# An encoder-decoder layer: two score pieces ahead of a visit's values, and the values' bank in a ring of eight

## The chip, the core and the metric

The kernel runs on one NeuronCore of one Trainium2 chip. The metric is the device time of one launch in microseconds. All arithmetic is fp32. The engines that matter here are TensorE (PE in the profile, with its weight loads as PEld), VectorE (DVE), ScalarE (ACT), GpSimd (POOL), and the DMA queue that SyncE (SP) issues.

## What is computed

One transformer layer with an encoder over a short context (2 sequences of 77 rows) and a decoder over 2 sequences of 2048 rows, width 512, 16 heads of 32. The part that the change touches is the decoder's causal self-attention:

```python
yn = _ln(y, dec_n1_s, dec_n1_b)
y = y + _mha(yn, yn, dec_sa_in_w, dec_sa_in_b, dec_sa_out_w, dec_sa_out_b, sb)
# inside _mha, for each head:
scores = einsum('bhqd,bhkd->bhqk', q, k) / sqrt(hd) + bias     # bias holds the causal mask
attn = softmax(scores, axis=-1)
out = einsum('bhqk,bhkd->bhqd', attn, v)                       # then out @ w_out.T + b_out
```

After it come cross-attention to the encoder's 77 rows and a feed-forward part of width 2048. The kernel does these last two in a second stage, and computes several of the large products there and the key and value projections by a seven-product scheme of half-size blocks.

## The kernel before, in words

**Units.** Self-attention is cut into units `(b, m, g, t)`: batch `b` (2), block `m` of 512 rows (4), group `g` of four heads (4), and tile `t` of 128 query rows in the block (4). A unit has `i = 4m + t` key tiles before its own, so it works on `i + 1` tiles of 128 keys: 1 to 4 in block 0, 5 to 8 in block 1, 9 to 12 in block 2, 13 to 16 in block 3. Units run in the order of the tuple.

**Pieces and visits.** `pieces(i)` (L315) cuts the key tiles of a unit into pieces of at most four. The main loop (L1730 to L1756) takes up to two pieces of one unit at a time; this text calls one such turn of the loop a visit. A unit of block 1 has one visit, a unit of blocks 2 and 3 has two. In block 3 both visits have two pieces; in block 2 the second visit has one.

**What a visit does.** The steps are, in program order:

- `turn(pair)` (L410): for every key tile ("load" in the code) four 128x128 transposes of the probabilities, one per head, into one PSUM bank (PE, L424), and a copy of that bank to one of eight SBUF tiles `pts`. The first half of the copies goes to ACT (L430), the second half to DVE (L428). One exponential is emitted behind the fourth load, and one at the end.
- `slot(n + 1)`, at a unit's last visit only: the jobs that a table has for the next unit: projections of queries, keys and values of the next block, the output projection `out_job` of the block before, and norms. A job is typically 8 or 16 matmuls.
- one score piece (`scores`, L357): four matmuls in row groups, one per head, each into its own bank (PE, L374), and then four evictions by DVE that write the raw scores to SBUF and take their maximum (L383), or add the bias for the last two tiles of a unit (L390). After a unit's last piece DVE makes the negated maximum `nm` (L399), and the four exponentials of the unit are put into a list, `late_exps`.
- `exps(k)`: emits up to `k` exponentials from that list to ACT (L404); `k` is 2 in block 1 and 1 in blocks 2 and 3.
- `values` (L435): for every key tile of the visit four matmuls in column groups (PE, L441).
- the remaining score pieces that are allowed (`while may_score()`).

Which scores are allowed follows from `may_score`: the probabilities of unit `n` overwrite those of unit `n - 2`, so a piece of unit `n + 2` may be scored as soon as unit `n` has been transposed that far. In block 3 that is two pieces at each visit, and the last piece of unit `n + 2` belongs to the second visit of unit `n`.

**Order on the engines.** The schedule is written out by hand: each engine's instructions run in the order in which the code emits them, and semaphores hold an instruction until its operands are ready. So an instruction that waits on ACT holds all that stands behind it on ACT.

**PSUM.** There are eight banks. Seven of them go round in `bank()` (L179): transposes, jobs and scores take the next one in turn, whatever it was used for last, and wait until its last reader is done. The eighth, bank 7, belongs to `values`: the four tiles `t` of a group accumulate there over all their key tiles, and when the last is done the whole bank (128x512) is copied to an SBUF tile `oT` (L447), by DVE for blocks 1 to 3. Six `oT` tiles go round; `out_job` reads four of them per block.

Of the kernel before, what the change touches and what calls it, by code (L numbers as in the profile page):

```python
# [12 lines left out]
ALU = mybir.AluOpType  # L13
# [4 lines left out]
P = 128  # L18
B, T, S, D = 2, 2048, 77, 512
H, HD, DFF = 16, 32, 2048  # L20
NC = D // P
NF = DFF // P
HC = P // HD
MB = 512
NMB = T // MB
TB = MB // P
# [28 lines left out]
def tile_encoder_decoder(ctx: ExitStack, tc: tile.TileContext, ins, out):  # L55
    nc = tc.nc
    x, src = ins["x"], ins["ctx_1024"]
# [101 lines left out]
    with (  # L159
# [14 lines left out]
        oT_all = ac.tile([P, 6, TB * P], F32, name="oT")  # L174
        bo = ac.tile([P, D], F32, name="row_dec_sa_out_b")
        psum = ps.tile([P, 8, 512], F32, name="psum")
        count = {"bank": 0, "banks": 7, "pts": 0, "oT": 0, "mm": 0}

        def bank():  # L179

            i = count["bank"] % count["banks"]
            count["bank"] += 1
            return psum[:, i, :]

        def in_turn(what, tile):
            i = count[what] % tile.shape[1]
            count[what] += 1
            return tile[:, i, :]

        def rows4(r):  # L190
            return slice(r * HD, (r + 1) * HD)
# [54 lines left out]
        def out_job(b, m, t):  # L246
            def run(w):
                x1 = xr.pop((b, m, t))
                mm = bank()
                for c in range(NC):  # L250
                    nc.tensor.matmul(  # L251
                        mm, ots[b, m, c][:, ts(t, P)], w[:, c, :], start=(c == 0), stop=(c == NC - 1)
                    )
                nc.vector.tensor_tensor(x1, mm, x1, ALU.add)
                nc.sync.dma_start(y1[b][m][:, t, :], x1)

            return lambda: big_w("o"), run, False
# [10 lines left out]
        def residual(b, m, t):  # L268
            residual_load(b, m, t)
            residual_add(b, m, t)  # L270
# [139 lines left out]
        def turn(pieces):  # L410

            first = units[pieces[0][0]][1] == 0
            loads = []
            for n, k0, kn in pieces:
                ks = range(k0, k0 + kn)
                if first:
                    loads += [[(n, k, r) for k in ks] for r in range(HC)]
                else:
                    loads += [[(n, k, r) for r in range(HC)] for k in ks]
            for o, load in enumerate(loads):  # L420
                pt = bank()
                pts = in_turn("pts", pts_all).rearrange("p (x q) -> p x q", q=P)
                for x, (n, k, r) in enumerate(load):
                    nc.tensor.transpose(pt[:, ts(x, P)], state[n]["p"][r][:, k], ident)  # L424
                    got[n, k, r] = pts[:, x, :]
                w = len(load) * P
                if o % 2 if first else o >= (len(loads) + 1) // 2:
                    nc.vector.tensor_copy(pts[:, : len(load), :], pt[:, :w])  # L428
                else:
                    nc.scalar.copy(pts[:, : len(load), :], pt[:, :w])  # L430
                if not first and o == min(3, len(loads) - 1):
                    exps(1)
            exps(HC if first else 1)

        def values(n, k0, kn):  # L435
            b, m, g, t = units[n]
            i = m * TB + t
            for k in range(k0, k0 + kn):
                ot = psum[:, 7, :].rearrange("p (t q) -> p t q", q=P)
                for r in range(HC):  # L440
                    nc.tensor.matmul(  # L441
                        ot[rows4(r), t, :], vv[:, k, ts(g * HC + r, HD)], got.pop((n, k, r)),
                        start=(k == 0), stop=(k == i),
                    )
                if t == TB - 1 and k == i:
                    o = ots[b, m, g] = in_turn("oT", oT_all)
                    (nc.vector.tensor_copy if m else nc.scalar.copy)(o, psum[:, 7, :])  # L447

        ri_of = [const.tile([P, RB], F32, name=f"ri{i}") for i in range(2)]
        for t in ri_of:  # L450
# [617 lines left out]
        for x, (b, m) in enumerate(blocks):  # L1068
            u = x * NU
            first = m == 0  # L1070

            if first:
                jobs[max(u - 5, -1)].append(q_job(b, m, 0))
                jobs[max(u - 4, -1)].append(k_job(b, m, 0))
                for t, at in enumerate((u + 1, u + 2, u + 3, u + 4) if x else (-1, 1, 3, 4)):
                    jobs[at].append(v_job(b, m, t))
                jobs[u - 1 if x else 0].append(q_job(b, m, 1))
                jobs[u if x else 2].append(k_job(b, m, 1))
                for g, at, then in ((2, 3, 4), (3, 5, 6)) if x else ((2, 6, 7), (3, 8, 9)):
                    jobs[u + at].append(q_job(b, m, g))  # L1080
                    jobs[u + then].append(k_job(b, m, g))
            else:
                (late if x == 1 else light)[u - 5].append(lambda b=b, m=m: token_sums(b, m))
                todo = {
                    -5: "q0", -4: "k1 k6", -3: "k7 k4", -2: "k2 k5", -1: "k3 v1", 0: "v6 v7", 1: "v4 v2", 2: "q1",
                    3: "v5 v3", 4: "q2", 5: "q3",
                } if x > 1 else {
                    -4: "q0 k1", -3: "k6 k7", -2: "k4 k2", -1: "k5 k3", 0: "v1 v6", 1: "v7 v4 v2", 2: "q1",
                    3: "v5 v3", 4: "q2", 5: "q3",
                }  # L1090
                for at, names in todo.items():
                    for name in names.split():
                        i = int(name[1])
                        jobs[u + at].append(q_job(b, m, i) if name[0] == "q" else part_job(name[0], b, m, i))
            if x == 0:
                jobs[NU + 5].append(fold_job())
            for t in range(TB):
                end = x == len(blocks) - 1
                jobs[u + NU + (2 if end else 7) + t].append(out_job(b, m, t))
                if not end:  # L1100
                    light[u + NU + 6 + t].append(lambda b=b, m=m, t=t: residual(b, m, t))
                elif t < 2:
                    light[u + NU - 1].append(lambda b=b, m=m, t=t: residual(b, m, t))
                if x:
                    held = x == 1 and t >= 2
                    light[u - NU + 5 + t].append(lambda b=b, m=m, t=t, held=held: norm_load(b, m, t, held))
                    ahead[u - NU + 6 + t].append(lambda b=b, m=m, t=t: norm_stats(b, m, t))
                    ahead[u - NU + 6 + t].append(lambda b=b, m=m, t=t: norm_center(b, m, t))
                    turned_at = 10 + t // 2 if x == 1 else u - NU + 7 + t
                    light[turned_at].append(lambda b=b, m=m, t=t: norm_turn(b, m, t))  # L1110
            for g in range(NC):
                apart = not (x == len(blocks) - 1 and g >= NC - 2)
                d = spread(b, m, g) if apart else divide(b, m, g)
                for k in range(4 if apart else 2):
                    light[u + g * TB + TB + k].append(lambda d=d: next(d, None))
                at = u + g * TB - 3
                light[max(at, -1)].append(lambda b=b, m=m, g=g: load_bias(b, m, g))
# [602 lines left out]
        def score_next():  # L1720
            n, k0, kn = stream[at[0]]
            scores(n, k0, kn)
            scored_to[n] = k0 + kn
            at[0] += 1
# [5 lines left out]
        while i < len(stream):  # L1730
            n = stream[i][0]
            pair = [p for p in stream[i : i + 2] if p[0] == n]
            while scored_to.get(n) != size[n]:
                score_next()
            while any(u == n for u, _ in late_exps):
                exps(1)
            ends = pair[-1][1] + pair[-1][2] == size[n]
            if ends:
                for f in ahead[n + 1]:
                    f()  # L1740
            turn(pair)
            if n == end - 2:
                for _, k0, _ in pair:
                    feed(k0 + 4)
            turned_to[n] = pair[-1][1] + pair[-1][2]
            if ends and n + 1 < end:
                slot(n + 1)
            if may_score():
                score_next()
            exps((0, 2, 1, 1)[units[n][1]])  # L1750
            for p in pair:
                values(*p)
            while may_score() and (len(pair) > 1 or units[n][1] == 0):
                score_next()
            i += len(pair)
# [2 lines left out]
        for t in (2, 3):  # L1758
            residual_load(*blocks[-1], t, pts_all[:, 2 * t - 3, :])
        late_loads()  # L1760
        count.update(bank=0, banks=4)
        side = cross(1)
        slot(end)
        for s in range(4):
# [58 lines left out]
```

## Time and profile before

| | us |
|---|---|
| median of three runs (2784.79 to 2785.24) | 2784.84 |
| the profiled execution | 2785.57 |
| its span, first to last instruction | 2783.8 |

| engine | busy us | share of the span | instructions |
|---|---|---|---|
| PE | 2757.1 | 99% | 26294 |
| PEld | 2137.0 | 77% | 26294 |
| DVE | 1885.9 | 68% | 5412 |
| ACT | 1439.6 | 52% | 2761 |
| POOL | 915.2 | 33% | 777 |

A row of the timeline holds the start and the length in us, the engine, the line of the kernel, the operation with what it writes and reads, a count where like instructions are merged, and in brackets how long the engine was idle before it and what released it. Matmuls overlap in their pipeline and their ends are modelled, so PE's busy time hides short waits. What a group of matmuls costs is read from its start to the start of the next group. Self-attention takes the time to about 1700 us of the span, the second stage the rest.

### The profile page before, as it was taken

What the parts mean: (1) busy time and instruction counts of PE and PEld (TensorE: products, weight loads), DVE (VectorE), ACT (ScalarE), POOL (GpSimd) and SP (SyncE); (2) the same over time, 40 slices, a digit from 0 to 9 for tenths busy, and PEclk for the clock granted to TensorE, in tenths of its full rate; (3) what the DMA queues carried; (4) which work ended last, traced back from release to release, by engine and by line L of the source; (5) the groups of instructions that cost most, each with busy time, mean ns of one, the idle gap of its engine ahead of it and who ended that gap; (6) DMA issues with size and microseconds to landing.
All of it is one profiled execution on the core that took longest, in us unless ns stands there. A gap on an engine that the chain in (4) does not pass through costs nothing. (4 is left out here: it accounts for less than half of the span.)

```text
span 2783.8 us, 66824 instructions
## 1 busy us (share of the span) xinstructions
PE 2757.1 (99%) x26294; PEld 2137.0 (77%) x26294; DVE 1885.9 (68%) x5412; ACT 1439.6 (52%) x2761; POOL 915.2 (33%) x777
## 2 busy tenths in 40 slices
PE   9999999999999999999999999999999999999998
PEld 5577776677666566676677667898989898989898
DVE  5676587788887578687788895555555646464645
ACT  3544455656666556666656665434444444444431
POOL 1501134400100412212300002364646474746456
PEclk9999999999999999999999999999999999999999
DMA  7423345421112521233211004574748575656475
GB/s 224 140 88 110 111 129 161 128 59 38 38 55 58 142 76 55 89 100 103 96 55 40 25 32 138 182 236 155 230 155 233 179 224 162 221 163 222 147 227 182
DMA packets 282252, 362.45 MB, mean 130 GB/s; under 512 B 39073, under 2 KB 156625, under 8 KB 281811
## 3 DMA queue, kind: packets, MB, share of 16 engines
q1 hardware_dynamic: 281938, 358.18, 42.0%
q8 instruction: 208, 3.41, 0.5%
q14 instruction: 106, 0.86, 0.1%
HBM read 314.49 MB, written 43.59 MB: 129 GB/s over the span
## 5 line engine op out<-in xcount | busy, mean ns | idle before, releaser
L404 ACT ACTIVATE pp<-pp,nm 128x128 f32<-128x128 f32 (+15 forms) x512 | 612.1, 1202 | 143.8 <-DVE nm L399 139.3
L383 DVE TENSOR_SCALAR_CACHE_REDUCE pp<-psum 128x512 f32<-128x512 f32 (+3 forms) x1024 | 558.9, 591 | 59.1 <-PE psum L374 57.4
L424 PEld LDWEIGHTS psum<-ident,pp 128*128 128x128 f32 x4352 | 475.8, 142 | 110.0 <-DVE pp L383 56.0
L430 ACT COPY pts<-psum 128x512 f32<-128x512 f32 (+3 forms) x592 | 300.9, 576 | 474.1 <-PE psum L424 342.8
L424 PE MATMUL psum<-ident,pp 128*128 128x128 f32 x4352 | 538.3, 278 | 7.6 <-ACT nT L310 2.3
L428 DVE COPY pts<-psum 128x512 f32<-128x512 f32 (+2 forms) x544 | 330.1, 660 | 65.8 <-PE psum L424 65.1
L374 PE MATMUL psum<-kT,q 32*128 32x512 f32 (+3 forms) x2560 | 358.7, 574 | 3.8 <-DVE pp L383 1.9
L441 PEld LDWEIGHTS psum<-pts,vv 128*32 128x32 f32 x8704 | 225.8, 110 | 126.0 <-issue 115.6
L1523 PE MATMUL psum<-pp 128*128 128x128 f32 x2560 | 304.5, 276 | 1.9 <-POOL pp L936 1.6
L1523 PEld LDWEIGHTS psum<-pp 128*128 128x128 f32 x2560 | 296.3, 192 | 8.6 <-issue 2.8
L441 PE MATMUL psum<-pts,vv 128*32 128x128 f32 x8704 | 279.5, 275 | 2.4 <-DVE pts L428 1.7
L936 POOL TENSOR_TENSOR pp<-pp 128x512 f32<-128x512 f32 x159 | 212.7, 1354 | 128.1 <-DMA pp<-in_dec_ff_wT_dram 68.9
L1494 PE MATMUL psum<-vv,pp 128*128 128x256 f32 x1024 | 236.2, 381 | 0.0
L374 PEld LDWEIGHTS psum<-kT,q 32*128 32x128 f32 x2560 | 122.8, 183 | 122.8 <-issue 79.6
L1494 PEld LDWEIGHTS psum<-vv,pp 128*128 128x128 f32 x1024 | 190.5, 190 | 25.6 <-issue 0.5
L390 DVE CUSTOM_DVE_ANT_0 pp<-psum,bias 128x256 f32<-128x256 f32 (+1 forms) x512 | 196.1, 411 | 15.7 <-PE psum L374 15.6
L1507 DVE TENSOR_TENSOR kT<-kT,psum 128x512 f32<-128x512 f32 x96 | 65.8, 686 | 190.7 <-PE psum L1494 190.6
L1494 PE MATMUL psum<-nT,pp 128*128 128x256 f32 x768 | 174.1, 380 | 0.0
L1510 ACT ACTIVATE kT<-kT,vecs 128x256 f32<-128x256 f32 x192 | 87.0, 501 | 156.7 <-DVE kT L1507 156.0
L1494 PEld LDWEIGHTS psum<-nT,pp 128*128 128x128 f32 x768 | 144.3, 190 | 20.2 <-issue 1.6
L469 POOL TENSOR_TENSOR oT<-rirows,oT 128x512 f32<-128x512 f32 x30 | 38.3, 1275 | 368.9 <-DMA rirows<-rec 214.2
L1531 ACT COPY oT<-psum 128x128 f32<-128x128 f32 x56 | 14.9, 267 | 239.2 <-PE psum L1523 239.2
(242 smaller groups left out, 3908.5 us busy)
## 6 DMA issues: line engine op xcount, KB each, us to landing
pp<-w_d SPq DMA_DIRECT2D x520, 256.0 KB
pp<-in_dec_ff_wT_dram SPq DMA_DIRECT2D x112, 256.0 KB
wqk<-in_dec_sa_in_wT_dram SPq DMA_DIRECT2D x76, 256.0 KB
bias<-tzg SPq DMA_DIRECT2D x128, 128.0 KB
pp<-wo_d SPq DMA_DIRECT2D x56, 256.0 KB
vv<-in_enc_ff_wT_dram SPq DMA_DIRECT2D x8, 1024.0 KB
xr<-in_x_dram SPq DMA_DIRECT2D x32, 256.0 KB
vv<-y SPq DMA_DIRECT2D x32, 256.0 KB
```

The source lines that it names most:

```text
L374: nc.tensor.matmul(banks[r][:, : kn * P], q[rows4(r), ts(t, P)], kT[rows4(r), g, k0 * P : (k0 + kn) * P], start=True, stop=True,)
L383: nc.vector.tensor_scalar(p[:, k0 : k0 + far], s[:, :far], 1.0, None, ALU.mult, ALU.max, accum_out=st["mx"][:, r, c : c + 1],)
L390: nc.vector.tensor_tensor_reduce(p[:, k0 + far : i + 1], s[:, far:kn], near[:, 2 - (kn - far) :], 1.0, LOWEST, ALU.add, ALU.max, accum_out ...
L404: nc.scalar.activation(p, p, AF.Exp, bias=nm, accum_out=to)
L424: nc.tensor.transpose(pt[:, ts(x, P)], state[n]["p"][r][:, k], ident)
L428: nc.vector.tensor_copy(pts[:, : len(load), :], pt[:, :w])
L430: nc.scalar.copy(pts[:, : len(load), :], pt[:, :w])
L441: nc.tensor.matmul(ot[rows4(r), t, :], vv[:, k, ts(g * HC + r, HD)], got.pop((n, k, r)), start=(k == 0), stop=(k == i),)
L936: engine.tensor_tensor(out, a, b, ALU.subtract)
L1494: nc.tensor.matmul(mm[:, ts(f, TOK)], a[:, c, ts(f, P)], b[:, c, :], start=fresh and f == 0 and c == 0, stop=c == 1, skip_group_check=True,)
L1510: nc.scalar.activation(dst[:, e, :], src[:, e, :], AF.Relu, bias=vec("dec_ff1_b", f + e))
L1523: nc.tensor.matmul(psum[:, bank_i, ts(col, P)], lhs[:, c, :], w[:, c, :], start=fresh and k in (0, 3) and c == 0, stop=c == 3, skip_group_ ...
```

## The change

There are four edits and a few that follow from them.

1. **Two score pieces in a row.** At a visit with two pieces in blocks 1 to 3, up to two score pieces are emitted ahead of `exps(k)` and `values`, where there was one. The other visits keep one.
2. **The ring has eight banks, and the values take theirs from it.** `values` now takes a whole visit. It takes the bank that has been longest in the ring, sums that visit's key tiles there, and gives the bank back to the end of the ring once the eviction is emitted. Block 0 still holds one bank for the four tiles of a group, and copies it as 128x512.
3. **Sums beside PSUM.** In blocks 1 to 3 a visit's sum is evicted as 128x128: the first visit of a unit by a copy on ACT into the `oT` tile, the second by DVE, which adds it there. One unit per block, `(g, t) = (2, 0)`, holds its bank over both visits and is copied once, on ACT.
4. **Copies of a visit with eight loads.** ACT takes six of the eight copies (all but loads 4 and 6), where it took four. The exponential that stood behind the fourth load stands behind the eighth. Other lengths stay as they were.

The output projections of a block other than the last in its batch move one slot earlier (slots 6 to 9 of the next block where they were 7 to 10), and so does the residual's load and its addition on POOL.

```diff
-        count = {"bank": 0, "banks": 7, "pts": 0, "oT": 0, "mm": 0}
+        count = {"pts": 0, "oT": 0, "mm": 0}
+        ring = list(range(8))
 
         def bank():
-            i = count["bank"] % count["banks"]
-            count["bank"] += 1
-            return psum[:, i, :]
+            ring.append(ring.pop(0))
+            return psum[:, ring[-1], :]
...
                 w = len(load) * P
-                if o % 2 if first else o >= (len(loads) + 1) // 2:
+                if o % 2 if first else o in (4, 6) if len(loads) == 8 else o >= (len(loads) + 1) // 2:
                     nc.vector.tensor_copy(pts[:, : len(load), :], pt[:, :w])
                 else:
                     nc.scalar.copy(pts[:, : len(load), :], pt[:, :w])
-                if not first and o == min(3, len(loads) - 1):
+                if not first and o == (7 if len(loads) == 8 else min(3, len(loads) - 1)):
                     exps(1)
             exps(HC if first else 1)
 
-        def values(n, k0, kn):
+        sums_held = {}
+
+        def values(pair):
+            n, k0, _ = pair[0]
             b, m, g, t = units[n]
             i = m * TB + t
-            for k in range(k0, k0 + kn):
-                ot = psum[:, 7, :].rearrange("p (t q) -> p t q", q=P)
+            k1 = pair[-1][1] + pair[-1][2]
+            whole = m == 0
+            key = (b, m, g) if whole else n
+            begun = key in sums_held
+            if not begun:
+                sums_held[key] = ring.pop(0)
+            v = sums_held[key]
+            ot = psum[:, v, ts(t, P)] if whole else psum[:, v, :P]
+            keep = t < TB - 1 if whole else (g, t) == (2, 0) and k1 <= i
+            for k in range(k0, k1):
                 for r in range(HC):
                     nc.tensor.matmul(
-                        ot[rows4(r), t, :], vv[:, k, ts(g * HC + r, HD)], got.pop((n, k, r)),
-                        start=(k == 0), stop=(k == i),
+                        ot[rows4(r)], vv[:, k, ts(g * HC + r, HD)], got.pop((n, k, r)),
+                        start=k == k0 and (whole or not begun), stop=k == k1 - 1 and (whole or not keep),
                     )
-                if t == TB - 1 and k == i:
-                    o = ots[b, m, g] = in_turn("oT", oT_all)
-                    (nc.vector.tensor_copy if m else nc.scalar.copy)(o, psum[:, 7, :])
+            if keep:
+                return
+            if (b, m, g) not in ots:
+                ots[b, m, g] = in_turn("oT", oT_all)
+            o = ots[b, m, g]
+            if whole:
+                nc.scalar.copy(o, psum[:, v, :])
+            elif k0 == 0 or begun:
+                nc.scalar.copy(o[:, ts(t, P)], ot)
+            else:
+                nc.vector.tensor_tensor(o[:, ts(t, P)], ot, o[:, ts(t, P)], ALU.add)
+            ring.append(sums_held.pop(key))
...
-                jobs[u + NU + (2 if end else 7) + t].append(out_job(b, m, t))
+                out_at = u + NU + (2 if end else 7 if m == NMB - 1 else 6) + t
+                jobs[out_at].append(out_job(b, m, t))
                 if not end:
-                    light[u + NU + 6 + t].append(lambda b=b, m=m, t=t: residual(b, m, t))
+                    (light if x else late)[out_at - 1].append(lambda b=b, m=m, t=t: residual(b, m, t))
...
-            if may_score():
-                score_next()
+            for _ in range(2 if len(pair) > 1 and units[n][1] else 1):
+                if may_score():
+                    score_next()
             exps((0, 2, 1, 1)[units[n][1]])
-            for p in pair:
-                values(*p)
+            values(pair)
             while may_score() and (len(pair) > 1 or units[n][1] == 0):
                 score_next()
...
-        count.update(bank=0, banks=4)
+        assert len(ring) == 8
+        ring[:] = range(4)
```

## The prediction

> **What bounds the kernel now.** I read the page's engine busy times first, then the busy times by stretches of 100 us, the waits of PE's weight loads, and the timeline of blocks 2 and 3.
>
> ```profile
> PE 2757.1 (99%) x26294; PEld 2137.0 (77%) x26294; DVE 1885.9 (68%) x5412; ACT 1439.6 (52%) x2761; POOL 915.2 (33%) x777
> 800.00:900.00 100.00, 99.78 (x1262) 70.51 (x1263) 74.95 (x241) 65.89 (x107) 1.27 (x1) 1.00 0.16 44
> PEld psum L424 <- DVE pp L383: 56.0, 93, 0.8
> PEld psum L374 <- ACT pts L430: 3.7, 19, 0.2
> ```
>
> PE bounds it, and the change removes no matmul. So it can only win or make waits of PE. These hide inside the modelled matmul times, so I compare each PE group's start-to-start time with the shortest of its kind. In self-attention the excess sums to 65 us of 1700, nearly all of it in 91 places of over 0.15 us (the first at 23.6, the last at 1697.3). That is the most there is to win. Here is block 2:
>
> ```profile
> 424.92 0.71 PE L374 MATMUL psum<-kT,q 32*128 32x256 f32 x8
> 425.56 0.86 PE L441 MATMUL psum<-pts,vv 128*32 128x128 f32 x24
> 425.65 0.43 DVE L390 CUSTOM_DVE_ANT_0 pp<-psum,bias 128x256 f32<-128x256 f32 x1
> 426.36 3.71 PE L424 MATMUL psum<-ident,pp 128*128 128x128 f32 x32
> 427.35 1.26 ACT L404 ACTIVATE pp<-pp,nm 128x1152 f32<-128x1152 f32 x1 [3.97 <-DVE nm L399]
> 428.61 2.02 ACT L430 COPY pts<-psum 128x512 f32<-128x512 f32 x4
> 430.00 1.81 PE L374 MATMUL psum<-kT,q 32*128 32x512 f32 x8
> 430.68 0.30 PEld L374 LDWEIGHTS psum<-kT,q 32*128 32x128 f32 x4 [0.20 <-ACT pts L430]
> 431.74 1.95 PE L441 MATMUL psum<-pts,vv 128*32 128x128 f32 x64
> 433.62 1.14 PE L374 MATMUL psum<-kT,q 32*128 32x512 f32 x8
> 434.70 1.97 PE L424 MATMUL psum<-ident,pp 128*128 128x128 f32 x16
> 434.78 0.69 DVE L383 TENSOR_SCALAR_CACHE_REDUCE pp<-psum 128x512 f32<-128x512 f32 x1 [1.06 <-PE psum L374]
> 437.23 1.28 DVE L428 COPY pts<-psum 128x512 f32<-128x512 f32 x2
> ```
>
> A unit's last piece is scored at 424.92, ahead of its visit's values. DVE evicts it, and the first exponential of that unit starts at 427.35, when `nm` is there. It stands on ACT ahead of the next turn's copies, whose banks filled from 426.36 on, so they start at 428.61. At 430.68 two of the next score matmuls still wait for a bank that ACT has not copied, and the values start at 431.74, 1.74 us behind that piece instead of the 1.08 us that the piece at 433.62 takes.
>
> In block 3 this does not happen, because the last piece comes behind the values and `exps` ahead of them:
>
> ```profile
> 706.64 1.30 PE L441 MATMUL psum<-pts,vv 128*32 128x128 f32 x40
> 707.87 0.93 PE L374 MATMUL psum<-kT,q 32*128 32x384 f32 x8
> 709.18 0.29 DVE L383 TENSOR_SCALAR_CACHE_REDUCE pp<-psum 128x128 f32<-128x128 f32 x1
> 709.42 2.06 ACT L430 COPY pts<-psum 128x512 f32<-128x512 f32 x4 [5.54 <-PE psum L424]
> 711.73 1.90 ACT L404 ACTIVATE pp<-pp,nm 128x1920 f32<-128x1920 f32 x1 [0.25 <-DVE nm L399]
> 723.74 4.63 PE L424 MATMUL psum<-ident,pp 128*128 128x128 f32 x32
> 724.39 0.42 DVE L383 TENSOR_SCALAR_CACHE_REDUCE pp<-psum 128x256 f32<-128x256 f32 x1
> 727.47 2.00 ACT L404 ACTIVATE pp<-pp,nm 128x2048 f32<-128x2048 f32 x1 [0.93 <-DVE nm L399]
> 728.30 1.27 PE L374 MATMUL psum<-kT,q 32*128 32x512 f32 x8
> 729.47 1.99 ACT L404 ACTIVATE pp<-pp,nm 128x2048 f32<-128x2048 f32 x1
> 729.50 1.95 PE L441 MATMUL psum<-pts,vv 128*32 128x128 f32 x64
> 731.39 1.14 PE L374 MATMUL psum<-kT,q 32*128 32x512 f32 x8
> 732.46 3.33 PE L424 MATMUL psum<-ident,pp 128*128 128x128 f32 x28
> ```
>
> ACT copies at 709.42 as soon as banks fill, and the exponential (711.73) comes behind the copies. What is lost here is small: the turn at 723.74 waits 0.9 us for DVE's banks (4.56 to 728.30, against 3.64 from 426.36 to 430.00).
>
> The Trainium skill (Perfetto Trace Analysis, Identifying the Most-Contended Engine) judges PE's headroom by LDWEIGHTS busy time and calls matmul busy time a bad measure. By it the stretch above has 30% to win and a gain of hundreds of us would be open. The rows disagree: a run of values without a wait (64 matmuls, 729.50 to 731.39) repeats to 0.01 us, so I keep 65 us as the ceiling.
>
> **The change, part by part.**
>
> *Two score pieces in a row, block 3.* At the second visit of unit n both pieces of unit n + 2, the last one included, now come ahead of `exps(1)`. The list is empty then (three of the unit's four exponentials go out at each first visit), so the first exponential of n + 2 is emitted there, ahead of the next turn's copies, as in block 2. Of eight loads six copies are ACT's, and the next two pieces take the turn's eight banks in order, so they wait for these copies. The chain from the first piece A of a second visit to the values V of the next visit, for 16 key tiles:
>
> - A's start to its first eviction 1.16 (433.62 to 434.78), four evictions 2.45 (434.78 to 437.23), the last piece's evictions to the exponential 3.08 (724.39 to 727.47), the exponential 2.00;
> - four copies to the bank of head 3, 2.06, and 0.05 to the matmul (430.63 to 430.68); then two pieces of 1.07, behind which copies 5 and 7 (2 x 0.52) are just in time: 2.14.
>
> The sum is 12.9 us. Applied to the row at 424.92, with one piece: 0.73 + 1.70 + 1.26 + 2.02 + 0.05 + 1.07 = 6.83, measured 6.82. PE's own work on that way is two pieces 2.14, values of six tiles 1.45 (between 1.23 for five at 706.64 and 1.88 for eight), the turn 3.64, two pieces 2.14: 9.4. So PE waits 3.5 us. In the same way n + 2 of 15 tiles: last piece 2.55 (709.18 to 711.73), exponential 1.9, 12.3 against 8.9, 3.4 us; of 14 (last piece of two tiles 1.70, 425.65 to 427.35; exponential 1.8): 11.4 against 9.4, 2.0 us; of 13 (pieces of three and two tiles, 0.95 + 1.9 + 1.7 + 1.7 + 4.25): 10.5 against 8.9, 1.6 us. A batch has 4, 4, 3 and 3 of these: 14.0 + 13.6 + 6.0 + 4.8 = 38 us, two batches **+77**. Jobs do not cover it: they stand between the turn and A, ahead of the chain.
>
> *The visit after.* ACT then runs three exponentials, the 0.27 us sum copy and the second visit's copies. PE reaches its pieces after values and a turn of five to eight loads. I work this out to 0.5 to 1.7 us of wait where slot n + 1 has no job (9 slots in all), else a 3.5 us job covers it: **+10**. Block 1 emits two exponentials behind the fresh `nm`; jobs cover that, except at slot 10, which loses its output projection to slot 6: **+5**.
>
> *What goes.* The second of two pieces in a row waits for the first one's bank, because the ring has seven:
>
> ```profile
> 403.48 3.04 PE L374 MATMUL psum<-kT,q 32*128 32x512 f32 x16
> 1458.29 3.03 PE L374 MATMUL psum<-kT,q 32*128 32x512 f32 x16
> 1461.25 0.98 PE L424 MATMUL psum<-ident,pp 128*128 128x128 f32 x7
> 465.13 2.71 PE L374 MATMUL psum<-kT,q 32*128 32x512 f32 x8
> 467.77 0.43 PE L441 MATMUL psum<-pts,vv 128*32 128x128 f32 x8
> 469.30 5.37 PE L424 MATMUL psum<-ident,pp 128*128 128x128 f32 x32
> 474.60 0.71 PE L374 MATMUL psum<-kT,q 32*128 32x512 f32 x4
> ```
>
> 2.96 us instead of 2.14, 14 times (the first and last rows): 11. Where DVE is late (465.13, 1.6 us; 469.30, 1.7 us), its lead and its relief help. Of block 2's 29 us in both batches I take 21 as gone (the 0.7 us waits like that at 430.00 stay), of block 3's 10 all, of block 1's 11 half: **-36**. The bounds are -11 (the ring alone) and -65 (all).
>
> *Copies and sums.*
>
> ```profile
> L1531 ACT COPY oT<-psum 128x128 f32<-128x128 f32 x56 | 14.9, 267 | 239.2 <-PE psum L1523 239.2
> L1539 DVE TENSOR_TENSOR oT<-psum,oT 128x128 f32<-128x128 f32 x56 | 15.7, 281 | 0.0
> L447 DVE COPY oT<-psum 128x512 f32<-128x512 f32 x24 | 16.4, 685 | 1.0 <-PE psum L441 1.0
> ```
>
> 72 visits have eight loads, so 144 copies (0.64 us on DVE, half of the pair at 437.23; 0.52 on ACT) move: DVE -92, ACT +75. The sums put 96 x 0.267 = 26 on ACT, 60 x 0.281 = 17 on DVE, and take 24 x 0.685 = 16 from it. No engine gets full, and what these cost in order is in the chains, so they count nothing more. A visit's sum needs the bank of head 0 of its first piece, evicted 1.8 us after that piece starts; the values start after 2.14. If DVE is late there, PE waits that long.
>
> *Moved jobs.* The output projections, residual loads on SP's queue and POOL's additions go together one slot earlier and keep their lead of a slot; only slot 10 is priced, above.
>
> Sum: 77 + 10 + 5 - 36 = +56 on the profiled execution's 2785.57, which stands 0.7 above the median: **2841**.
>
> **Rivals.**
>
> - *Faster.* PE does not wait in block 3, because the first exponential's `nm`, with DVE relieved, is early enough for the copies. Then only the -36 stays: 2749. For it: block 2 pays only 0.7 us in the same place. Against it: the chain fits that place to 0.01 us, and it has no DVE copy in it. It decides below 1.3 us a visit (36/28), where I have 2.75. The Trainium skill (PSUM — Partial Sum Buffer, Engine vs sequencer instructions) says that ScalarE's queue is strict FIFO. By it 2841, without it 2749; the copies at 428.61 agree with it.
> - *ACT binds in block 3.* The delay never drains, so the second wait (1.1 us) comes at all 32 units, not at 9, and only 20 us is gained: 77 + 35 + 5 - 20, 2882. For it: a 16-tile unit has 4 x 2.0 + 12 x 0.52 + 0.27 = 14.5 us on ACT against 15.5 on PE. Against it: most units have 3.5 us of jobs.
> - *No difference.* The waits are about half as long and balance the gain.
>
> **Numbers.** Forecast 0.65, at 2800 (all 65 won) to 2875; ACT binds 0.10; faster 0.20; no difference 0.05. Faster or slower by 0.2% (5.6 us) is about what can be told here, so 0.20, 0.05 and 0.75. The range goes from 2750, with half of the faster case, to 2880.
>
> **What would show it.** In block 3's timeline: an exponential of a new unit ahead of six ACT copies at each first visit, and score pieces of 4 to 5.5 us in a row instead of 2.14, released by ACT pts L430; that wait of PE's weight loads well above 3.7. Groups of 16 score matmuls at 2.14 in block 2. I am wrong if block 3 shows its copies ahead of the exponentials, or if PE's pieces wait for DVE instead.

## The result, and the profile after

| kernel | median us | ratio to before (95%) | block 1 | block 2 | block 3 |
|---|---|---|---|---|---|
| before | 2784.79 | | 407.3 | 469.7 | 526.7 |
| after | 2858.26 | 1.0264 (1.0253 to 1.0275) | 405.6 | 461.9 | 604.2 |

The medians are those of five executions each. The change makes the kernel 73.5 us slower; the forecast was 56 us slower. A block's column is the time from the first transpose of its units to the first of the next block's, summed over the two batches, in the profiled execution (2854.09 us, the fastest of the five, 68.5 above that of before). Blocks 1 and 2 gain 9.5 us, and block 3 loses 77.5.

The engine line and the waits of PE's weight loads after the change (tile and line, then what released them: sum in us, count, and the longest one):

```profile
PE 2794.0 (98%) x26294; PEld 2197.1 (77%) x26294; DVE 1807.6 (63%) x5304; ACT 1530.9 (54%) x3001; POOL 915.3 (32%) x777
```

```profile
PEld psum L452 <- DVE pp L383: 71.9, 97, 1.5
PEld psum L374 <- ACT pts L430: 54.3, 193, 2.0
PEld psum L424 <- DVE pp L383: 17.9, 53, 0.8
```

DVE lost 78 us of work and ACT got 91; the prediction's terms add up to 91 and 101. The wait of the score matmuls' weight loads for ACT's copies rose from 3.7 to 54.3 us, which is the wait named in advance. The first row, values (now L452) that wait for an eviction of scores, was named but not priced; experiment 1 shows that it costs PE next to nothing.

Block 3's timeline shows the chain, once with a unit of 16 key tiles next (645.84) and once with one of 13 (667.40):

```profile
645.84 2.04 PE L374 MATMUL psum<-kT,q 32*128 32x512 f32 x16
647.81 1.52 PE L452 MATMUL psum<-pts,vv 128*32 128x128 f32 x48
649.25 4.18 PE L424 MATMUL psum<-ident,pp 128*128 128x128 f32 x32
652.32 0.17 DVE L399 TENSOR_REDUCE nm<-mx 128x4 f32<-128x20 f32 x1
652.59 2.00 ACT L404 ACTIVATE pp<-pp,nm 128x2048 f32<-128x2048 f32 x1 [6.95 <-DVE nm L399]
654.59 3.00 ACT L430 COPY pts<-psum 128x512 f32<-128x512 f32 x6
655.21 3.55 PE L374 MATMUL psum<-kT,q 32*128 32x512 f32 x16 [1.77 <-ACT pts L430]
658.69 1.96 PE L452 MATMUL psum<-pts,vv 128*32 128x128 f32 x64
667.40 1.60 PE L374 MATMUL psum<-kT,q 32*128 32x384 f32 x16
674.33 3.55 PE L374 MATMUL psum<-kT,q 32*128 32x512 f32 x16
677.81 1.96 PE L452 MATMUL psum<-pts,vv 128*32 128x128 f32 x64
```

ACT is idle for 6.95 us, because the exponential at its head waits for `nm`, while the turn that starts at 649.25 fills eight banks, six of which only ACT's copies behind it can free. From the first piece to the values is 12.85 us here (12.9 predicted), and 10.41 for 13 tiles (10.5 predicted). The pieces take 3.48 us, start to start, where two of them take 1.93 without a wait (the row at 655.06 below). The pieces of 4 to 5.5 us that were to show it appear in two parts: 1.77 us idle and a row of 3.55.

### The profile page after: what moved, and what is told of

Read it like the earlier page. It is cut to its first block, busy times and chain, and to the rows that moved or that the text cites. A ratio compares the mean times of both kernels' runs of the same rounds, so it can differ in the third digit from the quotient of the medians.

```text
span 2852.2 us, 67060 instructions
## 1 busy us (share of the span) xinstructions
PE 2794.0 (98%) x26294; PEld 2197.1 (77%) x26294; DVE 1807.6 (63%) x5304; ACT 1530.9 (54%) x3001; POOL 915.3 (32%) x777
## 4 chain that ended last, share of the span: by engine, by line
PE 91%; DVE 4%; ACT 2%; issue 2%; POOL 0%; DMA 0%; SPq 0%; POOLq 0%; ACTq 0%; DVEq 0%
PE psum L424 16%; PE psum L1515 14%; PE psum L1544 12%; PE psum L374 11%; PE psum L452 9%; PE psum L1038 5%; PE psum L215 4%; PE psum L251 4%; PE psum L1675 3%; PE psum L1632 3%; DVE pp L383 2%; PE psum L860 2%; PE psum L830 1%; PE psum L868 1%; PE psum L585 1%
## 5 line engine op out<-in xcount | busy, mean ns | idle before, releaser
L430 ACT COPY pts<-psum 128x512 f32<-128x512 f32 (+2 forms) x736 | 378.2, 588 | 180.3 <-PE psum L424 149.8
L374 PE MATMUL psum<-kT,q 32*128 32x512 f32 (+3 forms) x2560 | 380.3, 574 | 21.2 <-ACT pts L430 17.1
L428 DVE COPY pts<-psum 128x512 f32<-128x512 f32 (+3 forms) x400 | 249.9, 654 | 145.4 <-PE psum L424 142.0
L452 PEld LDWEIGHTS psum<-pts,vv 128*32 128x32 f32 x8704 | 234.2, 113 | 132.5 <-DVE pp L383 71.9
L452 PE MATMUL psum<-pts,vv 128*32 128x128 f32 x8704 | 290.0, 282 | 9.9 <-DVE pp L383 4.1
L374 PEld LDWEIGHTS psum<-kT,q 32*128 32x128 f32 x2560 | 172.1, 185 | 164.0 <-issue 59.0
L266 POOL TENSOR_TENSOR xr<-xr,row_dec_sa_out_b 128x512 f32<-128x512 f32 x30 | 38.2, 1273 | 329.7 <-DMA xr<-in_x_dram 267.2
```

What stands on the lines that cost most here:

```text
L374: nc.tensor.matmul(banks[r][:, : kn * P], q[rows4(r), ts(t, P)], kT[rows4(r), g, k0 * P : (k0 + kn) * P], start=True, stop=True,)
L452: nc.tensor.matmul(ot[rows4(r)], vv[:, k, ts(g * HC + r, HD)], got.pop((n, k, r)), start=k == k0 and (whole or not begun), stop=k == k1 - ...
```

## The experiments

**1. Keep the order, hold the exponentials back.** The list's length is taken before the pieces are scored, and `exps` emits no more than that. So a unit whose last piece was just scored starts its exponentials one step later, behind the next turn's copies. All else stays as in the change.

```diff
+            ready = len(late_exps)
             for _ in range(2 if len(pair) > 1 and units[n][1] else 1):
...
-            exps((0, 2, 1, 1)[units[n][1]])
+            exps(min(ready, (0, 2, 1, 1)[units[n][1]]))
```

> The changed kernel, but a visit emits ahead of its values only those exponentials that were in the list before its own score pieces. Order theory (the first exponential of a new unit, which waits for nm, stands ahead of the next turn's copies on ACT): block 3's waits go, its length falls from 307 and 297 us (both batches) to 255 to 272 and 240 to 255, and the time to 2760 to 2785. ACT-load theory (six copies of eight fill ACT): the copies stay, so at least 40 of the 73 us stay, 2825 or more.

Measured: 2779.27, ratio to before 0.9981 (0.9972 to 0.9991), 79 us below the change. Blocks 405.7, 460.9, 529.2: of the 74 us between the two profiled executions, block 3 has 75. The same place in its timeline, and the waits of PE's weight loads:

```profile
647.53 2.04 PE L374 MATMUL psum<-kT,q 32*128 32x512 f32 x16
649.50 1.52 PE L452 MATMUL psum<-pts,vv 128*32 128x128 f32 x48
650.94 4.18 PE L424 MATMUL psum<-ident,pp 128*128 128x128 f32 x32
651.64 2.05 ACT L430 COPY pts<-psum 128x512 f32<-128x512 f32 x4 [4.30 <-PE psum L424]
654.01 0.17 DVE L399 TENSOR_REDUCE nm<-mx 128x4 f32<-128x20 f32 x1
655.06 2.00 PE L374 MATMUL psum<-kT,q 32*128 32x512 f32 x16
655.64 2.00 ACT L404 ACTIVATE pp<-pp,nm 128x2048 f32<-128x2048 f32 x1
656.99 1.95 PE L452 MATMUL psum<-pts,vv 128*32 128x128 f32 x64
```

```profile
PEld psum L452 <- DVE pp L383: 66.7, 96, 0.8
...
PEld psum L424 <- DVE pp L383: 23.0, 79, 0.8
...
PEld psum L424 <- ACT pp L404: 15.1, 17, 2.7
...
PEld psum L374 <- ACT pts L430: 11.8, 68, 0.2
```

The copies start 0.7 us into the turn, the exponential comes behind them, and piece to values is 9.46 us. The prediction's 9.4 is met by terms that offset each other: the turn takes 4.12 us to the next piece where it has 3.64, and each pair of pieces some 1.95 where it has 2.14. Where one exponential of each unit stands on ACT is worth 79 us. The values' wait for DVE is nearly as long as in the change (66.7 against 71.9), though they follow two pieces after 1.93 us: it costs PE next to nothing. And the run shows what the rest of the change is worth without the wait for copies, gains less costs: 6 us.

**2. ACT's share of the copies.** Once under the order of the change (`e3_split4`) and once under the repaired order of experiment 1 (`e9_held_split4`), ACT goes back to four of eight copies.

```diff
-                if o % 2 if first else o in (4, 6) if len(loads) == 8 else o >= (len(loads) + 1) // 2:
+                if o % 2 if first else o >= (len(loads) + 1) // 2:
...
-                if not first and o == (7 if len(loads) == 8 else min(3, len(loads) - 1)):
+                if not first and o == min(3, len(loads) - 1):
```

> The changed kernel with the copies of eight loads split four and four as before, the exponential behind the fourth load. Order theory: the score pieces still wait for ACT's copy 3, which comes as late as before, so the time stays within 15 us of 2858. ACT-load theory: at least 40 us come back, 2818 or less.

> The kernel with the held exponentials (e1_held) and the copies split four and four. If six copies on ACT are what makes the score lead pay, it is slower than 2779 by 5 us or more; if ACT's six copies are too many once the order is right, it is faster by 3 us or more.

Measured: 2866.67 (1.0288, 1.0268 to 1.0309) and 2796.48 (1.004, 1.0026 to 1.0055). With less work on ACT the kernel is no faster than the change, and 8 us slower by the medians, though the two ranges overlap (2858.69 to 2870.00 and 2854.09 to 2860.52). So ACT's load is not what binds block 3. In the repaired order the six copies are worth 17 us.

**3. Two pieces in a row, and nothing else.** From the kernel before, with its ring of seven: the loop alone (`e4_two_alone`), then with experiment 1's hold as well (`e10_two_held`).

```diff
-            if may_score():
-                score_next()
+            for _ in range(2 if len(pair) > 1 and units[n][1] else 1):
+                if may_score():
+                    score_next()
```

> The kernel before with the two score pieces in a row alone: seven banks in the ring, bank 7 for the values, four copies each. Order theory: block 3 loses about what it loses in the whole change (77 us of length), and the second piece waits 0.8 us more for its bank at each of some 130 visits, partly inside those waits: 2850 to 2930. ACT-load theory: no more than 2810, since ACT has only four copies.

> The kernel before with two score pieces in a row and the held exponentials, seven banks in the ring. Order theory: of the 100 us that the two pieces alone cost, block 3's 75 go; what is left is the eighth bank's wait of 0.8 us at each pair of pieces: 2795 to 2830.

Measured: 2884.69 (1.0359, 1.0343 to 1.0374) and 2852.36 (1.0243, 1.0227 to 1.0258). Alone it costs 75 us in block 3, as much as in the change, with four copies on ACT. It also costs 17.5 and 8.1 us in blocks 1 and 2. With the hold I had expected at most 2830. It gives back 37 of block 3's 75 us, and blocks 1 and 2 stay 16 and 13 us longer than before. What stays is another wait:

```profile
650.26 2.82 PE L374 MATMUL psum<-kT,q 32*128 32x512 f32 x16
652.17 0.29 PEld L374 LDWEIGHTS psum<-kT,q 32*128 32x128 f32 x2 [0.75 <-DVE pp L383]
653.01 1.30 PE L441 MATMUL psum<-pts,vv 128*32 128x128 f32 x40
```

```profile
PEld psum L374 <- DVE pp L383: 52.2, 110, 1.4
```

With seven banks the second piece waits for the first one's evictions by DVE. `e9_held_split4` differs from this kernel by the ring of eight, the sums and the moved jobs, and is 56 us faster; this wait is 6.9 us there, over 19 places. So two pieces in a row need the eighth bank, and it is worth much more than the 11 us of the prediction.

**4. The other parts without two pieces in block 3.** `e2_single_in_3` keeps one piece ahead in block 3 and leaves the six copies. `e5_ring_alone` takes one piece everywhere and experiment 2's copies, so that the ring, the sums and the moved jobs are left.

```diff
-            for _ in range(2 if len(pair) > 1 and units[n][1] else 1):
+            for _ in range(2 if len(pair) > 1 and units[n][1] in (1, 2) else 1):    # e2_single_in_3
+            for _ in range(1):                                                      # e5_ring_alone
```

> The changed kernel, with two pieces in a row in blocks 1 and 2 only. Order theory: block 3 has its last piece behind the values again and costs what it cost before or a little less, 2765 to 2785 in all. ACT-load theory: 2825 or more, since the six copies stay.

> The changed kernel with one score piece ahead of the values everywhere and the copies split four and four: what is left is the ring of eight, the sums beside PSUM and the moved jobs. By the prediction's sum the ring alone is worth 11 us: 2770 to 2780. If the sums cost something in the order of ACT or DVE, 2785 or more.

Measured: 2794.92 (1.0037, 1.0022 to 1.0052), where 2765 to 2785 was expected, and 2782.18 (0.999, 0.9981 to 0.9999), between the two expectations. In the first, block 3 takes 546.7, 20 more than before. From a first visit's values to the second's it is 26 us longer than before, and a new wait of that size stands there, first as its sum, then in the timeline:

```profile
PEld psum L424 <- ACT oT L464: 26.2, 24, 1.5
```

```profile
659.90 0.25 ACT L464 COPY oT<-psum 128x128 f32<-128x128 f32 x1
660.20 1.97 PE L424 MATMUL psum<-ident,pp 128*128 128x128 f32 x16 [1.30 <-ACT oT L464]
```

The sum of a first visit leaves its bank by a copy of 0.25 us on ACT, and that copy stands behind the exponentials, which here stand behind six copies. The bank comes up in the ring while the next turn runs. In `e5_ring_alone` the blocks are 397.7, 475.4 and 525.0: the ring, the sums and the moved jobs gain 9.6 us in block 1, gain 1.7 in block 3 and lose 5.7 in block 2. No run isolates these 5.7 us, but the traces place most of them. The output projection that stood in slot 10 of block 2 (3.6 us of PE, L251) is in slot 6 now. Where it stood, behind unit (2, 1), PE waits 0.46 and 2.51 us (523.82 and 526.66) for the next unit's last exponentials, and from this unit's first values to the next unit's it takes 4.3 us longer than before, both batches together, although the projection is no longer in it.

**5. The hold in the kernel before, and a mix by blocks.** `e7_before_held` is experiment 1's hold in the kernel before. `e11_two_in_2` is experiment 1 with two pieces in a row and six copies in block 2 alone; blocks 1 and 3 take one piece and four copies. `e12_two_exps` is the latter with two exponentials at the end of each turn of block 2, in place of one.

```diff
+            six = len(loads) == 8 and units[pieces[0][0]][1] == 2
...
-                if o % 2 if first else o in (4, 6) if len(loads) == 8 else o >= (len(loads) + 1) // 2:
+                if o % 2 if first else o in (4, 6) if six else o >= (len(loads) + 1) // 2:
...
-            for _ in range(2 if len(pair) > 1 and units[n][1] else 1):
+            for _ in range(2 if len(pair) > 1 and units[n][1] == 2 else 1):
...
-            exps(HC if first else 1)
+            exps(HC if first else 2 if units[pieces[0][0]][1] == 2 else 1)    # e12_two_exps only
```

> The kernel before with the exponentials held. Only block 2 has an exponential that waits for nm ahead of the copies: its waits of 0.7 to 1.0 us, seven in each batch, go, so 5 to 12 us less, 2773 to 2780. If PE then waits for DVE's copies in the same places, nothing changes.

> The changed kernel with two pieces in a row, and six copies on ACT, in block 2 alone; blocks 1 and 3 have one piece and four copies each; exponentials are held as in e1_held. The lengths of the blocks in e5_ring_alone (blocks 1 and 3) and e1_held (block 2), less those of the kernel before, add to about 20 us: 2762 to 2772 if the blocks are independent, 2775 to 2785 if what one block wins the next gives back.

> The kernel e11_two_in_2, with two exponentials instead of one at the end of each turn in block 2. At 520.33 and 521.78 of its trace PE waits 3.4 us for a unit's own last two exponentials, which stand behind four norm activations on ACT; the same comes once in the second batch, and the other units of block 2 wait 0.4 to 0.8 us in that place. If these waits are only a matter of order, 6 to 14 us go: 2753 to 2761. If the earlier exponentials hold the next copies instead, as in block 3 of the changed kernel, 2767 or more.

Measured: 2786.76 (1.0007, 0.9998 to 1.0016), 2767.13 (0.9935, 0.9923 to 0.9948) and 2767.21 (0.9936, 0.9922 to 0.9949). The hold alone does nothing for the kernel before: I had expected 5 us or more in block 2, which moved by 0.9. Transposes that wait for a unit's own exponentials went from 1.8 us over 4 places to 12.7 over 18, so the exponentials that were held come late for the unit's own turn. The mix lands where it was expected, with blocks of 397.7, 460.4 and 525.1, each the length that its own setting had in another kernel. It is the fastest version, 17.6 us below the kernel before. What still stands in block 2 is the wait for a unit's last exponentials, and the attempt on it moved that wait without shortening it (the mix, then the two exponentials a turn; the transposes are L425 here, one line further down):

```profile
518.71 1.48 ACT L404 ACTIVATE pp<-pp,nm 128x1408 f32<-128x1408 f32 x1
520.16 1.47 ACT L404 ACTIVATE pp<-pp,nm 128x1408 f32<-128x1408 f32 x1
520.33 0.33 PE L425 MATMUL psum<-ident,pp 128*128 128x128 f32 x1 [2.45 <-ACT pp L404]
521.78 4.93 PE L425 MATMUL psum<-ident,pp 128*128 128x128 f32 x29 [1.12 <-ACT pp L404]
```

```profile
519.43 1.48 ACT L310 ACTIVATE nT<-psum,vecs 128x128 f32<-128x128 f32 x4
519.58 0.33 PE L425 MATMUL psum<-ident,pp 128*128 128x128 f32 x1 [1.06 <-ACT pp L404]
520.80 1.47 ACT L404 ACTIVATE pp<-pp,nm 128x1408 f32<-128x1408 f32 x1
522.42 5.01 PE L425 MATMUL psum<-ident,pp 128*128 128x128 f32 x29 [2.51 <-ACT pp L404]
```

Emitting one exponential earlier let it pass, but the last one now stands behind four activations of a norm job, and PE's two waits add up to the same 3.57 us.

**6. The clock.** In the change, PE's granted clock halves for 44 us of block 3 in all. This kernel fills the waits there: the eighth load of the first visits is transposed 3 to 6 times more, into the same bank with the same result. It does more work; the copy of that load then waits for the last of the transposes.

```diff
+                if len(loads) == 8 and o == 7 and units[pieces[0][0]][1] == 3 and pieces[0][1] == 0:
+                    for _ in range((3, 6, 6, 3)[units[pieces[0][0]][3]]):
+                        for x, (n, k, r) in enumerate(load):
+                            nc.tensor.transpose(pt[:, ts(x, P)], state[n]["p"][r][:, k], ident)
```

> The changed kernel, and in block 3 PE repeats the transposes of the eighth load of a first visit 3 times (tiles 0 and 3) or 6 times (tiles 1 and 2), 1.3 and 2.6 us of work that only fills the wait for ACT's copies. If the half-clock stretches after these waits come from PE standing still, most of them go in block 3 and the time falls by 8 to 20 us although PE does more. If the waits themselves are all of the loss, the time is equal or a little above 2858.

Measured: 2850.12 (1.0235, 1.022 to 1.025), 8 us below the change, with more matmuls (5.6 between the profiled executions). Block 3 falls from 604.2 to 599.7. The same stretch of the change and of this kernel (busy time and count of PE, PEld, DVE, ACT and POOL, then the granted clock):

```profile
700.00:800.00 100.00, 95.83 (x980) 67.38 (x979) 65.83 (x220) 58.86 (x96) 16.78 (x13) 0.93 0.13 38
```

```profile
700.00:800.00 100.00, 98.38 (x1138) 73.01 (x1135) 69.63 (x234) 64.36 (x105) 16.75 (x13) 1.00 0.13 38
```

The granted clock goes from 0.93 to 1.00, and no half-rate stretch is left in block 3. What the half clock costs is seen by visits. These are the times between the starts of two visits' values in block 3, summed over both batches, worked out from the timelines:

| kernel | second visit to the next unit's first | first visit to second |
|---|---|---|
| before | 215.9 | 300.5 |
| change | 278.6 | 313.0 |
| exponentials held (1) | 212.7 | 302.5 |
| waits filled (6) | 282.5 | 302.1 |

The way from first to second visit is 10.5 us longer in the change than with the exponentials held, and filling the waits takes away all of it: that is half clock. On the other way the six places with the most excess (4.0 to 5.1 us) fall to 3.0 to 3.4, together by 8.5 us. So the half clock costs some 19 us of the 75. The filling itself takes some 12 of them at other places of the table, where PE had little or no wait to fill, and 2.6 more ahead of the blocks' first values.

## Why the prediction was right, and where it was not

**Bound and direction: right.** PE stays the bound, the time comes from block 3, and it comes by the step that was named. The chain's price holds at 16 and 13 tiles within 0.1 us where the clock is full.

**Two pieces in block 3, +77: the price right, the count too high.** The table's first column holds the named chain: 66 us over experiment 1, of which 8.5 are half clock, so 57. With the clock full a place costs 3.4 us for 16 tiles, 2.8 to 3.3 for 15, 1.8 for 14 and 1.6 for 13, where I had 3.5, 3.4, 2.0 and 1.6. But I let all 14 places of a batch pay in full. A block's first place pays nothing, and at a few (the one at 814.0 pays 0.6) PE waits in experiment 1 as well.

**The visit after, +10: half of it, though its column reads 10.5.** The column's 10.5 is half clock, and together with the chain's 8.5 that makes 19 us, which the sum did not have. The wait itself is there, but in experiment 1 too, so the table does not show it. Where a job stands ahead of the pieces PE has no wait, as I had it. At six visits with pieces and no job the pair takes up to 2.97 us where it takes 1.97 behind a job (2.96 from 1675.70 to 1678.66 in the change, released by ACT's copies; 2.83 in experiment 1). In all that is 4 to 5 us.

**Block 1, +5: too small, and hidden by another term.** Two pieces, with the six copies, cost 8 us there (405.7 against 397.7 in `e5_ring_alone` and `e11_two_in_2`), and the ring with the sums and the moved jobs gains 9.6, where I took 5.

**What goes, -36: the step that failed.** Some 20 us went. Block 1 gained the 9.6. Block 2 gained 7.8 in the change and 8.8 in experiment 1, where I took 21. Block 3 is 2.5 longer than before in experiment 1; less the 4 to 5 us of the visit after, that is a gain of about 2, where I took 10. The 6 us of experiment 1 are these gains less its costs. I took a wait of before as gone when its cause was gone. Transposes that wait for DVE did fall, from 56.0 us to 17.9 in the change and 23.0 in experiment 1, but others stand close behind. In experiment 1 a unit's own exponentials are waited for 15.1 us over 17 places, where it was 1.8 over 4 (the hold alone makes it 12.7), and ACT's copies 11.8 us, where it was 3.7. In block 2 the moved jobs add to this. I priced the projection that leaves slot 10 in block 1 alone, but in block 2 unit (2, 1), whose waits it had covered, takes 3.2 us longer than before in the change and 5.7 in experiment 1, both batches together. How the rest of block 2's shortfall is divided among these waits is not shown. The rival that the change is faster, at 2749, would have been about 2779 with its condition met, as in experiment 1.

**Copies and sums, nothing: wrong.** No engine got full, as said, but six copies instead of four are worth some 8 us in the change and 17 in the repaired order, and with six copies and one piece in block 3 the sum copy's place behind the exponentials cost 20 us of the block (`e2_single_in_3`). The eighth bank, which I put at 11 us with two pieces in a row, is by the wait that fell from 52.2 to 6.9 us the larger part of 56.

**The total.** Between the profiled executions the costs come to about 88 us (57 and 19 for the chain and the half clock, 4 to 5 and 8), close to the sum's 92, though 19 of them are a term that it did not have and the chain is 20 below its 77: that part of the agreement is luck. The gains are about 20 instead of 36. So 2841 stood 17 under the measured 2858, of which some 5 are the distance of the median from the profiled execution. Of the rivals, "ACT binds" falls with experiment 2.

## What to carry to other kernels

Before moving work ahead in program order, list what it releases on the in-order engines, and ask what comes to stand at the head of a queue with an operand that is not there yet. Here an exponential that waited 7 us for its maximum held six copies of 0.5 us each, and letting it be emitted one step later gave back 79 us. When a sum of small waits is to be won, do not count a wait as gone until the next releaser in the trace is shown to be earlier; and set such a knob per stage, since the blocks here kept their own lengths in the mix.

## What the runs showed of the hardware that was not expected

Waits of under 2 us can halve PE's clock, depending on where they fall:

```profile
708.76 3.92 PE L424 MATMUL psum<-ident,pp 128*128 128x128 f32 x32
714.35 5.24 PE L374 MATMUL psum<-kT,q 32*128 32x512 f32 x16 [1.67 <-ACT pts L430]
719.51 2.79 PE L452 MATMUL psum<-pts,vv 128*32 128x128 f32 x48
```

These are rows of the change. The turn's work ends at 712.4 (708.76 and 3.64 for a full turn), PE then waits some 1.9 us, and the score matmuls follow one row group at a time as their banks come free. By the trace's clock records the half rate starts at 715.8 and lasts 6.8 us; block 3 has seven such stretches (six of 6.8 us, one of 3.4), 44 us in all. The values of 48 matmuls take 2.79 us in it instead of 1.52 (647.81). All stretches of half clock in the trace last about 3.4 or 6.8 us, the kernel's end apart.

The length of the wait does not decide it. PE is idle as long at 655.21 (1.77 us) and keeps its full clock there; of 26 places of block 3 with the wait, seven are followed by half clock. The clock records show a grid: the half-rate stretches start a whole number of steps of 3.413 us apart (715.816 and 739.710, seven steps; 715.816 and 1521.362, 236 steps). The wait ahead of 714.35 lies in one step, from 712.38 to 715.79, in which PE is busy 1.74 us. The wait ahead of 655.21 lies across two, in which PE is busy 2.47 and 2.56 us. Of all steps in block 3 of the change, the five in which PE is busy least (1.6 to 1.9 us) are each followed by half clock; the other two stretches follow steps of 2.2 and 2.4 us. It is not the whole rule: in `e4_two_alone` some steps with as little (1.73 us from 1636.96) are not followed by it.

The Trainium skill (TensorE: Matmul & The Clock Gate, Why this matters for your kernels) advises no idle gaps of PE over about 3 us. The Trainium skill's Part 1 on the same page describes a window of about 3.4 us, and the steps of 3.413 us agree with it. The gap here is 1.9 us, so the advice is too generous for this kernel. The Trainium skill's section there, "A second HAM failure mode: psum-queue depth-cycling", describes short idle times between groups of matmuls that make the clock swing; the rows above and experiment 6 agree with that.
